# Reordering the sums, the row maxima and the score products inside a fused transformer block's attention

## The chip, the core and the metric

One core of a Trainium2 chip runs the whole kernel in one launch. Its engines each work through a queue of their own, in order: TensorE (PE, with its weight loads PEld), VectorE (DVE), ScalarE (ACT), GpSimd (POOL), and SyncE (SP), which issues DMAs. The metric is the device time of one execution in microseconds; less is better.

## The reference

A transformer block with adaptive layer norm, in float32: batch 2, 2048 tokens, width 512, 16 heads of 32, hidden width 2048. Six shift, scale and gate vectors per batch row come from a condition; then

```
xm = layernorm(x) * (1 + sc_a) + sh_a
q, k, v = split(xm @ Wqkv)
scores = where(causal, q @ k.T * 32**-0.5, -inf)
x = x + gt_a * (softmax(scores) @ v @ Wproj + bproj)
xm = layernorm(x) * (1 + sc_m) + sh_m
x = x + gt_m * (gelu(xm @ W1 + b1) @ W2 + b2)
```

The softmax is exact: each query's own maximum is subtracted before the exponential.

## The kernel before

The two batch rows run one after the other through three stages: queries, keys and values (written to DRAM, read back in another layout); attention; projection of the attention's output. The feed-forward half follows for both. The first row's stages take about the times 0 to 210, 210 to 735 and 735 to 800 us, the second's 800 to 970, 970 to 1490 and 1490 to about 1560.

**Units.** Attention works in 16 units per row: four groups of four heads (`c`), and in each four blocks of 512 queries (`i`), in the order 0, 1, 2, 3 for the first group and 0, 2, 1, 3 for the others. A unit has 4i + 3 steps: one per 128 keys that lie wholly before the block, then three for the diagonal. The first diagonal step (number 4i) has one key tile, the second two tiles (384 and 128 queries wide), the third one.

**A step** (`scores_t`). TensorE puts minus the row maxima into four PSUM banks `st`, one per head (`st<-fold,sel`), and adds keys times queries (`st<-qst,kst`). ScalarE takes the exponentials into a tile `e` (four buffers, `E_BUFS`). In diagonal steps GpSimd zeroes the triangle above the diagonal with one `affine_select` per key tile (the masks). Two steps later (`LAG`) TensorE multiplies by the values (`o<-e,vv`).

**Row sums.** The `e` tiles of four whole steps are added by GpSimd into a chain tile `ee` (VectorE does it in the last unit); the tile of the first diagonal step is added to the last chain. TensorE sums chains and diagonal tiles over keys (`sm<-ee,ones`, `sm<-e,ones`), a chain four steps after its last tile.

**Maxima ahead of time.** The maxima have to be known before a unit starts, so the same scores are computed once more beforehand, with queries on partitions (`s<-kst,qst`), in units up to `AHEAD` = 3 ahead. `Row.todo` lists these score products; an item is one bank: a whole key block for one query tile, a single diagonal tile, or a pair of diagonal tiles (128 and 384 keys, or 256 and 256). `Row.score(n)` takes n items, singles first or, with `late`, pairs first, looking at the next eight; `Row.bank` issues the products and then VectorE's reductions into `mx` (`tensor_reduce`, L500, or a masked reduction, L495). The products go to a pool `ps_s` of two PSUM banks, or, with `borrow`, to one of the four `st` banks (`st<-kst,qst`). `due` says how many items each step takes.

When a unit's items are done, `Row.split` (L517 to L521, five short VectorE operations) splits the maxima into three bfloat16 parts `mhl`, with a score bank as scratch. `Row.rows` transposes these (`ps_m`, in a bank of `ps_s`) and VectorE spreads the transpose into `fold`.

**What sets the order.** `mm` and `act` keep an instruction where the code has it on its engine. Other instructions, VectorE's reductions, splits and folds among them, are placed by the scheduler, as are SyncE's DMAs. The last unit also prepares the projection (`prepare`: multiplications on VectorE, L467, and GpSimd, L465), and `finish` stores a unit's values and sums. `project_phase` then loads the sums back, inverts them, loads tokens (`xt`) and the attention's output (`at`), multiplies `at` by the inverted sums on GpSimd (L1265) and projects (`ps_o`). Weights for the feed-forward are loaded in between (`Pieces.load`, L1153).

## Time and profile before

| | |
|---|---|
| time, median of 3 runs | 2315.55 us (2315.52 to 2318.34) |
| profiled execution, its time / its span | 2314.76 us / 2313.0 us |
| TensorE busy | 2252.9 us, 97% |
| VectorE, ScalarE, GpSimd busy | 1443.8, 1006.2, 1021.5 us |
| mean granted TensorE clock | 0.996 |
| GpSimd: sums `ee` (L656) | 106 and 42, 4.58 us each |
| GpSimd: masks (L643) | 128, 0.66 us each |
| VectorE: reductions of 512 scores (L500) | 768, 0.68 us each |
| ScalarE: exponentials (L635) | 1152, 0.58 us each |

In the rows of the profile, `out<-in` are the program's tile names, and the idle time in brackets is that of the engine just before, with what ended it.

### The profile page before, as it was taken

How to read it: one execution, taken by the hardware profiler on the slowest of the kernel's cores; microseconds unless marked ns; L12 is line 12 of the kernel's file. 1: busy time of each engine (PE TensorE's matmuls, PEld its weight loads, DVE VectorE, ACT ScalarE, POOL GpSimd, SP SyncE). 2: the span in 40 equal slices, each digit the busy share in tenths (PEclk: the TensorE clock that was granted, in tenths of full speed). 3: DMA queues.
4: the chain of work that ended last, by engine and by line, in shares of the span. 5: the costliest groups of instructions: out<-in, count | busy, mean ns of one | idle time of the engine just before them, and what ended most of it. 6: DMA issues, size and time to landing. Idle time of an engine off the chain costs nothing.

```text
span 2313.0 us, 32545 instructions
## 1 busy us (share of the span) xinstructions
PE 2252.9 (97%) x12033; PEld 1374.5 (59%) x12033; DVE 1443.8 (62%) x3025; ACT 1006.2 (44%) x1952; POOL 1021.5 (44%) x561
## 2 busy tenths in 40 slices
PE   7999999999999999999999999999999999999998
PEld 5777555555544588755555554344684585486477
DVE  4677766767757667777577766662573483375366
ACT  4434555555555244355555556513313322332320
POOL 7252986877782692278777879340000000000000
PEclk9999999999999999999999999999999999999999
DMA  9877143231323796523223123272354253353433
GB/s 302 279 259 195 37 92 69 65 83 47 99 94 128 258 300 230 162 67 78 71 72 88 47 74 114 98 254 86 118 165 150 99 174 130 116 171 121 153 113 131
DMA packets 160505, 311.52 MB, mean 135 GB/s; under 512 B 16545, under 2 KB 48845, under 8 KB 158553
## 3 DMA queue, kind: packets, MB, share of 16 engines
q1 hardware_dynamic: 155488, 285.53, 40.9%
q0 software_dynamic: 4480, 23.36, 2.6%
q8 instruction: 95, 1.56, 0.3%
q14 instruction: 66, 0.53, 0.1%
q10 hardware_dynamic: 376, 0.55, 0.1%
HBM read 229.95 MB, written 87.29 MB: 137 GB/s over the span
## 4 chain that ended last, share of the span: by engine, by line
PE 84%; POOL 6%; DVE 5%; issue 2%; ACT 1%; DMA 1%; SPq 0%; POOLq 0%; DVEq 0%; ACTq 0%
PE ps_a L206 24%; PE st L206 16%; PE ps_b L206 12%; PE o L206 9%; PE s L206 8%; PE ps_c L206 6%; POOL ee L656 4%; PE sm L206 4%; PE ps_o L206 2%; DVE junk L495 2%; PE ps_xt L214 1%; DVE mx L500 1%; ACT e L635 1%; PE ps_o L214 1%; POOL e L643 0%
## 5 line engine op out<-in xcount | busy, mean ns | idle before, releaser
L635 ACT ACTIVATE e<-st 128x512 f32<-128x512 f32 (+1 forms) x1152 | 571.5, 578 | 392.9 <-PE st L206 370.6
L500 DVE TENSOR_REDUCE mx<-s 128x1 f32<-128x512 f32 x578 | 381.6, 686 | 223.0 <-PE s L206 221.9
L656 POOL TENSOR_TENSOR ee<-ee,e 128x2048 f32<-128x2048 f32 x106 | 485.8, 4583 | 16.3 <-ACT e L635 9.0
L206 PE MATMUL st<-qst,kst 128*128 128x512 f32 (+3 forms) x1280 | 412.4, 388 | 0.0
L206 PE MATMUL s<-kst,qst 128*128 128x512 f32 (+3 forms) x1054 | 381.2, 393 | 10.7 <-DVE mx L500 6.1
L206 PE MATMUL ps_a<-sum,w 128*128 128x256 f32 (+1 forms) x1088 | 346.6, 454 | 0.0
L206 PE MATMUL o<-e,vv 128*32 128x512 f32 (+3 forms) x2560 | 293.7, 540 | 9.4 <-POOL e L643 9.3
L206 PEld LDWEIGHTS st<-qst,kst 128*128 128x128 f32 x1280 | 230.0, 189 | 100.6 <-issue 67.6
L206 PEld LDWEIGHTS ps_a<-sum,w 128*128 128x128 f32 x1088 | 206.3, 190 | 109.8 <-issue 91.4
L495 DVE CUSTOM_DVE_ANT_0 junk<-s,causal 128x128 bf16<-128x128 f32 (+3 forms) x476 | 224.9, 472 | 65.0 <-PE s L206 51.3
L656 POOL TENSOR_TENSOR ee<-e 128x2048 f32<-128x2048 f32 x42 | 192.5, 4583 | 138.9 <-ACT e L635 130.8
L206 PEld LDWEIGHTS s<-kst,qst 128*128 128x128 f32 x1054 | 196.0, 188 | 70.5 <-DVE mx L500 21.7
L1615 DVE TENSOR_TENSOR h<-c,ps_b 128x512 f32<-128x512 f32 x32 | 22.0, 688 | 202.4 <-PE ps_b L206 202.4
L206 PEld LDWEIGHTS <-sel 32*128 32x128 bf16 x1152 | 29.4, 91 | 196.2 <-issue 196.2
L500 DVE TENSOR_REDUCE mx<-st 128x1 f32<-128x512 f32 x190 | 129.6, 682 | 0.4
L643 POOL TENSOR_SCALAR_AFFINE_SELECT e<-e 128x512 f32<-128x512 f32 x128 | 82.1, 663 | 91.8 <-ACT e L635 89.6
L1789 ACT ACTIVATE h<-h,cols 128x512 f32<-128x512 f32 x96 | 69.3, 722 | 120.4 <-DVE h L1615 120.4
L206 PE MATMUL ps_b<-sum,w 128*128 128x256 f32 (+1 forms) x384 | 120.6, 450 | 0.0
L206 PE MATMUL st<-fold,sel 32*128 32x512 bf16 (+1 forms) x1152 | 117.5, 374 | 2.8 <-DVE mx L495 1.7
L206 PEld LDWEIGHTS o<-e,vv 128*32 128x32 f32 x2560 | 57.8, 109 | 96.2 <-issue 64.3
L984 POOL TENSOR_TENSOR lo<-lo,hi 128x512 fp32r<-128x512 f32 x32 | 40.8, 1276 | 132.4 <-ACT hi L982 130.7
L206 PEld LDWEIGHTS ps_b<-sum,w 128*128 128x128 f32 x384 | 73.0, 190 | 37.2 <-issue 30.6
(206 smaller groups left out, 3094.7 us busy)
## 6 DMA issues: line engine op xcount, KB each, us to landing
kst<-k SPq DMA_DIRECT2D x128, 256.0 KB
qst<-q SPq DMA_DIRECT2D x128, 256.0 KB
w<-w1d SPq DMA_DIRECT2D x32, 896.0 KB
w<-w2d SPq DMA_DIRECT2D x28, 1024.0 KB
w<-w2d SPq DMA_DIRECT2D x28, 768.0 KB
q<-hi SPq DMA_DIRECT2D x32, 256.0 KB
q<-lo SPq DMA_DIRECT2D x32, 256.0 KB
k<-hi SPq DMA_DIRECT2D x32, 256.0 KB
```

The costliest lines, as they stand in the source:

```text
L206: return tc.keep_in_program_order(nc.tensor.matmul(*args, **kw))
L214: return tc.keep_in_program_order(nc.tensor.transpose(dst, src, ident[:n, :n]))
L495: nc.vector.tensor_tensor_reduce(junk[:, :w], x, causal[:, QB - w :], 1.0, MASKED, ALU.add, ALU.max, m,)
L500: nc.vector.tensor_reduce(m, x, axis=AX.X, op=ALU.max)
L635: act(nc.scalar.activation(e4[:, h, :w], sts[h][:, :w], AF.Exp))
L643: nc.gpsimd.affine_select(d, d, pattern=[[0, HC], [1, P]], compare_op=ALU.is_ge, fill=0.0, base=0, channel_multiplier=-1,)
L656: act(nc.gpsimd.tensor_tensor(dst, x, y, ALU.add))
L984: engine.tensor_tensor(lo, d, hi.bitcast(F32), ALU.subtract)
L1615: act(nc.vector.tensor_tensor(dst, x, y, ALU.add))
L1789: nc.scalar.activation(d, ps, AF.Gelu, bias=col(r_b1 + half * HF + f, 1))
```

## The change

In the attention's steps every VectorE operation of the scores is now kept in the order of the code (`vector`). The split is put off to the end of the step (`settle`) and takes a score bank of its own there. The sum of the first diagonal tile is issued one step later. `score` takes pairs when the next items are mostly pairs, and steps with mostly pairs place one product early instead of two (`two_parts`).

```diff
 def score(self, n, borrow=None, late=False):
-                first = pairs if late else singles
+                many = len(pairs) > len(singles)
+                first = singles if lent or not (late or many) else pairs
...
                 self.bank(*item, s)
                 if not self.todo or self.todo[0][0] != u:
-                    self.split(u, self.mx, s)
+                    self.unsplit.append((u, self.mx))
                     self.mx = None
-                    self.at += 1
+                    if not self.paced:
+                        self.settle(s)
+
+        def settle(self, s=None):
+            for u, mx in self.unsplit:
+                if s is None:
+                    s = ps_sp.tile([P, QB], F32, tag="s", name="s")
+                self.split(u, mx, s)
+                self.at += 1
+                s = None
+            self.unsplit = []
+
+        def vector(self, ins):
+            return act(ins) if self.paced else ins
...
+        def two_parts(self):
+            own = [item for item in self.todo[:8] if item[0] == self.todo[0][0]]
+            return sum(len(parts) for _, _, parts in own) > len(own) * 3 // 2
...
 def scores_t(u, step, n):
-                sts = []
+                sts, early = [], 0
...
-                    if h < 2 and n >= 3 or h >= HC - n and n < 3:
+                    if n < 3:
+                        if h >= HC - n:
+                            row.score(1)
+                    elif h == 0 or h == 1 and not row.two_parts():
                         row.score(1)
+                        early += 1
...
                     row.score(1, st_bank)
-                    row.score(min(n, HC) - 3, late=True)
+                    row.score(min(n, HC) - 1 - early, late=True)
...
 in the loop over steps
                         if last:
                             row.score(row.count(cum[-1], u + 1))
+                    row.settle()
+                    if u + 1 < len(units) and row.rows_made == u + 1:
                         make_rows = last or (ready > u + 1 and n_step >= 1)
...
                     row.score(max(0, len(row.todo) - rest))
+                    row.settle()
...
+                    if i and n_step == i * TQ + 1:
+                        add_to(u, chain, single)
...
                     elif i and n_step == i * TQ:
-                        add_to(u, chain, es)
+                        single = es
                         sums_of, wait = (chain, False), 2
```

The reductions (L495, L500), the split's five operations and the fold are wrapped in `self.vector(...)`; `paced` is set at the start of a row's attention.

GpSimd's queue at the end of the fourth unit of the first row, before (`e_3256` is the tile of the first diagonal step, `e_3297` of the second, `e_3324` of the third):

```order
L656 TENSOR_TENSOR ee_3165<-ee_3165,e_3213 128x2048
L643 AFFINE_SELECT e_3256<-e_3256 128x4x128
L656 TENSOR_TENSOR ee_3165<-ee_3165,e_3256 128x2048
L643 AFFINE_SELECT e_3297<-e_3297 128x4x128 x2
L643 AFFINE_SELECT e_3324<-e_3324 128x4x128
```

and now (`e_3259`, `e_3300`, `e_3328`):

```order
L694 TENSOR_TENSOR ee_3168<-ee_3168,e_3216 128x2048
L681 AFFINE_SELECT e_3259<-e_3259 128x4x128
L681 AFFINE_SELECT e_3300<-e_3300 128x4x128 x2
L694 TENSOR_TENSOR ee_3168<-ee_3168,e_3259 128x2048
L681 AFFINE_SELECT e_3328<-e_3328 128x4x128
```

The sum stands behind the two masks of the second step, in all 22 units of this kind.

VectorE's queue where a unit's maxima are split in the third unit, before (`s_2587` is the bank of the unit's last pair, `s_2601`, `st_2609` and `s_2612` belong to the next unit):

```order
L495 ISA junk_2592,mx_2467<-s_2587,causal_68 128x384
L517 TENSOR_REDUCE s_2587<-mx_2467 128x16
L520 TENSOR_TENSOR mhl0_87<-s_2587,mhl0_87 128x4x4
L500 TENSOR_REDUCE mx_2602<-s_2601 128x1
L521 TENSOR_TENSOR mhl0_87<-s_2587,mhl0_87 128x4x4
L500 TENSOR_REDUCE mx_2602<-st_2609 128x1
L495 ISA junk_2615,mx_2602<-s_2612,causal_68 128x128
```

and now (rows between the split's own are left out in both):

```order
L497 ISA junk_2593,mx_2468<-s_2588,causal_68 128x384
L503 TENSOR_REDUCE mx_2598<-s_2597 128x1
L503 TENSOR_REDUCE mx_2598<-st_2605 128x1
L497 ISA junk_2613,mx_2598<-s_2608,causal_68 128x384
L521 TENSOR_REDUCE s_2615<-mx_2468 128x16
L527 TENSOR_TENSOR mhl0_87<-s_2615,mhl0_87 128x4x4
L503 TENSOR_REDUCE mx_2598<-s_2641 128x1
```

The split stands behind the reductions of the step and uses a bank of its own, `s_2615`.

SyncE's queue at the end of the first row's attention, before (`o_145` and `sum_130` are the last unit's values and sums in DRAM, the `W` rows are feed-forward weights):

```order
L1240 DMA qst<-wide_135 128x2048
L684 DMA o_145<-ot 128x512
L683 DMA sum_130<-sums 4x512
L1153 DMA qst<-in_L_cond_W_dram 128x2x128 x4
L373 DMA r<-sum_130 128x16
L1225 DMA xt<-in_x_dram 128x512 x6
L1234 DMA at<-o_143 128x2048
```

and now:

```order
L1283 DMA qst<-wide_135 128x2048
L1196 DMA qst<-in_L_cond_W_dram 128x2x128 x3
L722 DMA o_145<-ot 128x512
L721 DMA sum_130<-sums 4x512
L1196 DMA qst<-in_L_cond_W_dram 128x2x128
L1196 DMA vv<-in_L_cond_W_dram 128x2x128 x3
L374 DMA r<-sum_130 128x16
L1268 DMA xt<-in_x_dram 128x512 x6
L1277 DMA at<-o_143 128x2048
```

Three weight loads stand ahead of the two stores, and three more ahead of the loads behind them; in the second row's attention these rows stand as before.

More of the change, by code (lines that the diff above doesn't have):

```diff
@@ L306, in __init__ @@
             self.mx = None
+            self.unsplit, self.paced = [], False
             self.spent = 0
@@ L494, in bank @@
                     junk = bp.tile([P, QB], BF16, tag="junk", name="junk")
-                    nc.vector.tensor_tensor_reduce(
-                        junk[:, :w], x, causal[:, QB - w :],
-                        1.0, MASKED, ALU.add, ALU.max, m,
+                    self.vector(
+                        nc.vector.tensor_tensor_reduce(
+                            junk[:, :w], x, causal[:, QB - w :],
+                            1.0, MASKED, ALU.add, ALU.max, m,
+                        )
                     )
                 else:
-                    nc.vector.tensor_reduce(m, x, axis=AX.X, op=ALU.max)
+                    self.vector(nc.vector.tensor_reduce(m, x, axis=AX.X, op=ALU.max))
                 self.spent += cost(w, last)
@@ L516, in split @@
             )
-            nc.vector.tensor_reduce(m, mx, axis=AX.X, op=ALU.max)
-            nc.vector.tensor_reduce(hl[:, :, :, 0], mx, axis=AX.X, op=ALU.max)
-            nc.vector.tensor_tensor(r, m, hl[:, :, :, 0], ALU.subtract)
-            nc.vector.tensor_tensor(hl[:, :, :, 1], m, hl[:, :, :, 0], ALU.subtract)
-            nc.vector.tensor_tensor(hl[:, :, :, 2], r, hl[:, :, :, 1], ALU.subtract)
+            for ins in (
+                lambda: nc.vector.tensor_reduce(m, mx, axis=AX.X, op=ALU.max),
+                lambda: nc.vector.tensor_reduce(hl[:, :, :, 0], mx, axis=AX.X, op=ALU.max),
+                lambda: nc.vector.tensor_tensor(r, m, hl[:, :, :, 0], ALU.subtract),
+                lambda: nc.vector.tensor_tensor(
+                    hl[:, :, :, 1], m, hl[:, :, :, 0], ALU.subtract
+                ),
+                lambda: nc.vector.tensor_tensor(
+                    hl[:, :, :, 2], r, hl[:, :, :, 1], ALU.subtract
+                ),
+            ):
+                self.vector(ins())
         def count(self, upto, last_unit):
@@ L569, in rows @@
             )
-            nc.vector.tensor_tensor(
-                fold[u % 2].rearrange("p (t q) -> p t q", t=TQ + 1),
-                ps.unsqueeze(1).to_broadcast([P, TQ + 1, P]),
-                tmask.unsqueeze(2).to_broadcast([P, TQ + 1, P]),
-                ALU.mult,
+            self.vector(
+                nc.vector.tensor_tensor(
+                    fold[u % 2].rearrange("p (t q) -> p t q", t=TQ + 1),
+                    ps.unsqueeze(1).to_broadcast([P, TQ + 1, P]),
+                    tmask.unsqueeze(2).to_broadcast([P, TQ + 1, P]),
+                    ALU.mult,
+                )
             )
@@ L586, in attention_phase @@
         b, vv, kst, qst = row.b, row.vv, row.kst, row.qst
+        row.paced = True
         with pool(f"att{b}") as ap, pool(
```

## The prediction

> **What bounds the kernel now.** I read the page first, for the engine that is full; then the table of waits cut down to TensorE; then the timelines of TensorE, GpSimd, VectorE and SyncE around its longest waits.

> ```profile
> PE 2252.9 (97%) x12033; PEld 1374.5 (59%) x12033; DVE 1443.8 (62%) x3025; ACT 1006.2 (44%) x1952; POOL 1021.5 (44%) x561
> PE o L206 <- POOL e L643: 9.3, 8, 2.4
> PE s L206 <- DVE mx L500: 6.1, 10, 1.2
> PE s L206 <- DVE mx L495: 3.8, 9, 1.4
> PE st L206 <- DVE mx L495: 1.7, 4, 0.4
> ```

> TensorE is busy for 97%, and the change takes no matmul away, so it can give back only what TensorE loses by waiting. The last four rows (engine and tile, what was waited for, total, times, longest) are the waits that the edits aim at: 9.3 us for GpSimd's masks, 11.6 us for VectorE's maxima. The nearly full engine leaves no third source inside the attention.

> The 9.3 us sit in four places: the end of the fourth unit and of the last unit but one, in both batch rows. The first and third, GpSimd and ScalarE ahead of TensorE, with the twins of the second row behind:

> ```profile
> 338.47 2.06 ACT L635 ACTIVATE e<-st 128x512 f32<-128x512 f32 x4 [1.31 <-PE st L206]
> 340.72 4.55 POOL L656 TENSOR_TENSOR ee<-ee,e 128x2048 f32<-128x2048 f32 x1
> 345.23 2.40 POOL L643 TENSOR_SCALAR_AFFINE_SELECT e<-e 128x512 f32<-128x512 f32 x4
> 345.92 1.64 PE L206 MATMUL o<-e,vv 128*32 128x384 f32 x16 [1.90 <-POOL e L643]
> 350.15 1.06 PE L206 MATMUL sm<-ee,ones 128*32 128x512 f32 x8
> 351.90 0.61 PE L206 MATMUL o<-e,vv 128*32 128x256 f32 x8
> ...
> 1106.75 1.07 PE L206 MATMUL o<-e,vv 128*32 128x384 f32 x16 [1.63 <-POOL e L643]
> 1111.18 0.61 PE L206 MATMUL o<-e,vv 128*32 128x256 f32 x8
> ...
> 680.07 2.06 ACT L635 ACTIVATE e<-st 128x512 f32<-128x512 f32 x4 [0.95 <-PE st L206]
> 682.80 4.56 POOL L656 TENSOR_TENSOR ee<-ee,e 128x2048 f32<-128x2048 f32 x1
> 688.00 1.93 PE L206 MATMUL o<-e,vv 128*32 128x384 f32 x16 [2.43 <-POOL e L643]
> 695.15 0.60 PE L206 MATMUL o<-e,vv 128*32 128x256 f32 x8
> ...
> 1447.27 1.07 PE L206 MATMUL o<-e,vv 128*32 128x384 f32 x16 [2.43 <-POOL e L643]
> 1450.46 1.90 PE L206 MATMUL sm<-ee,ones 128*32 128x512 f32 x8
> 1453.06 0.60 PE L206 MATMUL o<-e,vv 128*32 128x256 f32 x8
> ```

> (Start, length, engine, line, operation; in brackets the idle time before.) In the first place the four exponentials of the second diagonal step end at 338.47 + 2.06 = 340.53. GpSimd is free at 340.7, but its queue holds the 4.55 us sum next and the two masks behind it, so the value products stand until 345.9. The waits also drag the clock down:

> ```profile
> 344.00:352.00 8.00, 6.10 (x58) 3.50 (x61) 0.82 (x1) 3.55 (x8) 4.50 (x7) 0.79 1.00 208
> 684.00:696.00 12.00, 9.57 (x76) 3.94 (x72) 2.50 (x4) 4.37 (x10) 5.12 (x4) 0.72 0.06 23
> 1104.00:1112.00 8.00, 6.37 (x74) 3.48 (x73) 0.82 (x1) 4.27 (x9) 5.57 (x7) 1.00 0.95 210
> 1444.00:1454.00 10.00, 7.57 (x68) 3.08 (x66) 2.50 (x4) 4.39 (x9) 4.40 (x4) 0.83 0.07 28
> ```

> Each row is a stretch with its length and the engines' busy times; the third figure from the end is the granted clock: 0.21 of 8 us, 0.28 of 12 and 0.17 of 10 are 1.7, 3.4 and 1.7 us lost behind three of the four waits, none behind the shortest.

> **The change, part by part.** *The sum behind the masks.* Only the order on GpSimd changes: two masks (0.6 us each, 2.40 over four) pass the sum. In the first place they run from 340.7 to 341.9, before TensorE gets there at 345.92 - 1.90 = 344.02, so nothing is waited for. What is late next is the sum: 341.9 + 4.6 = 346.5. Its reader, the row-sum product at 350.15, moves forward. The undisturbed copy (1106.75 to 1111.18, at full clock) takes 4.43 us from the first value product to the next, so the first place runs 344.02 to 348.45 instead of 351.90: **3.45 us**. Its row sum falls 1.75 us ahead of that, by the copy's spacing as by these rows (351.90 - 350.15), at 346.7, just behind the sum. In the second place only the wait goes, 1.63 us.

> In the third and fourth places the sum ends at 682.8 + 1.2 + 4.6 = 688.6. TensorE is ready at 685.57 and wants the row sum, by the fourth place, 1450.46 - 1447.27 = 3.19 us later, less the half of 1.7 us of lost clock that falls there: 2.4, so at 688.0. A new wait of 0.6 us stays. The clean length there is 1453.06 - 1447.27 - 1.7 = 4.1. Third: 695.15 - 685.57 - 4.1 - 0.6 = **4.9**; fourth: 1453.06 - 1444.84 - 4.1 - 0.6 = **3.5**. Together **13.5 us** (8.4 of waits, less 1.2 new, and 6.3 of clock). The other 18 units have no such wait to lose, and the tightest of them is

> ```profile
> 472.91 2.07 ACT L635 ACTIVATE e<-st 128x512 f32<-128x512 f32 x4 [1.81 <-PE st L206]
> 483.38 1.06 PE L206 MATMUL sm<-ee,ones 128*32 128x512 f32 x8
> ```

> where the sum would end 1.2 + 4.6 us after the exponentials' 474.98, at 480.8, 2.6 us before its product. I take nothing there: the sum's delay lies in GpSimd's idle time, 56% of the span. Uncovered, 18 x 1.2 = 22 us. The tile of the moved sum is also held a step longer; the exponential that reuses it comes three steps on and has the same cover.

> [...]

> *VectorE's order, and the split last.* The split of the row maxima (L517 to L521) stood between reductions that free score banks:

> ```profile
> 275.33 0.18 DVE L517 TENSOR_REDUCE s<-mx 128x16 f32<-128x16 f32 x1
> 275.94 0.68 DVE L500 TENSOR_REDUCE mx<-s 128x1 f32<-128x512 f32 x1
> 276.54 0.18 DVE L521 TENSOR_TENSOR mhl<-s,mhl 128x16 bf16<-128x16 f32 x1
> 276.68 0.55 PE L206 MATMUL s<-kst,qst 128*128 128x128 f32 x2 [1.17 <-DVE mx L500]
> ```

> The split scribbles in the score bank that it was computed from, so that bank came free only at 276.6. Now it has a bank of its own, behind the step's reductions; the next product finds its bank at 275.3. I take the 1.17 us in both rows, 2.3 us, and 1.2 of the remaining 9 us: **3.5 us**. Bounds: all 11.6 us of the four rows' VectorE part above; below, a bank taken per split, of only two, 26 splits (13 units a row are scored inside the attention) of 1.4 us (275.33 to 276.72), 36 us. I stay near the upper rows since every split now has a step to finish in. The folds stand behind up to two more masked reductions; that too is in the lower bound.

> *Pairs spread.* The same instructions in other steps; TensorE's cost is nil either way, and VectorE's load evens out. Nothing taken beyond the 1.2.

> *The last unit* (VectorE sums there). The multiplication of the step now runs ahead of the sum:

> ```profile
> 727.88 4.45 DVE L659 TENSOR_TENSOR ee<-ee,e 128x512 f32<-128x512 f32 x4 [0.53 <-POOL e L643]
> 734.56 0.64 PE L206 MATMUL o<-e,vv 128*32 128x256 f32 x8 [0.27 <-POOL e L643]
> ```

> It half fills VectorE's 0.53 us of idleness, and 0.27 us of TensorE's is spare: a loss of 0.3 us per row (0 to 1.1), **-0.6**.

> *SyncE's queue, moved by the scheduler.* At the first row's end three weight loads now stand ahead of the stores of the last sums:

> ```profile
> 735.96 0.32 SPq L684 DMA_DIRECT2D o<-ot  x1
> 741.11 1.92 SPq L1153 DMA_DIRECT2D qst<-in_L_cond_W_dram  x4
> 743.12 0.41 SPq L373 DMA_DIRECT2D r<-sum  x1
> 746.42 0.43 SPq L1234 DMA_DIRECT2D at<-o  x1
> 755.14 1.27 POOL L1265 TENSOR_TENSOR at<-at,qst 128x512 f32<-128x512 f32 x1 [7.17 <-DMA at<-o]
> 765.50 1.27 POOL L1265 TENSOR_TENSOR at<-at,qst 128x512 f32<-128x512 f32 x1
> 764.01 3.94 PE L206 MATMUL ps_o<-kst,at 128*128 128x512 f32 x8
> ```

> Those loads wait for GpSimd until 741.11, so the two stores leave at about 742.6 and 743.0. Behind them now stand one weight load and three more (0.5 us each, by 1.92 for four), and the reload of the sums: 745.6 for 743.12, so the load `at<-o` slips by about 2.5 us, and GpSimd's first multiplication, which waited 7.17 us for it, with it. TensorE wants the fourth product of its block at 764.01 + 3 x 0.86 = 766.6, GpSimd ends the fourth chunk at 766.77: no cover. **-2.6 us** (0 if the bytes land sooner, 6.6 if the whole slip of the stores comes through).

> The sum: 13.5 + 3.5 - 0.6 - 2.6 = **13.8 us**. The profiled execution took 2314.8 us (1.8 around its span); the median, 2315.55, is 0.8 above. 2315.6 - 13.8 = **2301.8**.

> **The rivals.** *The clock stays.* If the half rate is not caused by these waits, or the 2.6 us at 766 brings it back, the 6.3 us go: 2301.8 + 6.3 = 2308.1. For: 1.63 us brought none, so it's no simple threshold. Against: three drops, three places, all of them right at the waits.

> *SyncE's stores cost their whole slip:* 6.6 and a half-rate stretch of 1.7 for 2.6, 2307.5. For: DMA is dense there and the load already ended a wait. Against: the old stores were early by far.

> *VectorE's written order holds TensorE.* In-order, a reduction waiting for its product holds up one that is ready, and each split turns over one of two banks. Every step that lends a bank could pay, and the lent products count them:

> ```profile
> L206 PE MATMUL st<-kst,qst x226: 388/396/453, 213.0 to 1430.8; 128*128 128x512 f32 x113
> ```

> At 0.1 us each that is 22.6 us, and no gain from VectorE, 2301.8 + 3.5 + 22.6 = 2327.9. It decides from (10.3 + 4.6)/226 = 0.066 us per step. For: VectorE is 62% busy, more in these steps. Against: TensorE's own order is the written one, so products come in the order in which they are reduced.

> *The wait only moves to the row sums.* If GpSimd is behind by 3 us more than these rows show, the four waits return as waits for the sum: about 2313.

> **How the numbers follow.** Chances: forecast 0.60, clock 0.12, SyncE 0.14, moved wait 0.07, written order 0.07. About 0.2%, 4.6 us, is what a measurement of this kernel tells from no change. The first three are faster by more than that: with 0.01 for mixtures on the border taken off, 0.85; the moved wait and the border are the same, 0.08; 0.07 slower. The range runs from 2296.5 (13.8, plus 3 of VectorE's further waits and 2.6 if the stores are free) to 2310.5, above both dearer cases; about 0.19 is left out.

> **What would show it.** In the profile after: no row of the value products waiting for GpSimd's masks but some tenths at the ends of rows; granted clock 1.00 in the four windows; a wait for the sum of at most 1 us in the third and fourth; the split behind the reductions and no 1.17 us wait; one wait of about 2.6 us for `at` at the first row's third projection block. I am wrong if waits for VectorE's maxima grow past 15 us, or the half rate is still there.

## The result, and the profile after

The changed kernel took 2304.05 us in the median of four runs (2301.64 to 2307.01), the kernel before 2315.53 us: a ratio of 0.9953, 95% interval 0.9934 to 0.9972, so 11.5 us faster (6.5 to 15.3 by the interval). Its profiled execution took 2301.64 us, its span is 2299.9 us, 13.0 us under that of before. The forecast was 13.8 us.

The table of TensorE's waits in the profile after (engine, tile, what was waited for; total, times, longest):

```profile
PE s L206 <- DVE mx L503: 2.8, 4, 1.1
PE ps_m L597 <- DVE mx L497: 2.0, 2, 1.0
PE s L206 <- DVE mhl L527: 1.5, 6, 0.3
...
PE sm L206 <- DVE ee L697: 1.3, 2, 0.6
PE ps_o L206 <- POOL at L1308: 1.2, 1, 1.2
...
PE s L206 <- DVE mx L497: 0.9, 1, 0.9
...
PE sm L206 <- POOL ee L694: 0.8, 2, 0.4
...
PE o L206 <- POOL e L681: 0.2, 1, 0.2
```

The waits for GpSimd's masks went from 9.3 us to 0.2, those for VectorE's maxima (`mx`, three rows, 11.6 us) to 3.7. What is left of these stood in before too: 1.08 us in the first unit of each row, 0.3 in unit 13, and one wait ahead of the attention (0.91 us, before 1.37). Four rows are new: the transposition `ps_m` waits for a reduction, and three waits for sums and for the projection's `at`. The first place of the masks, and the third, on GpSimd's and TensorE's timelines of the profile after:

```profile
338.28 1.80 POOL L681 TENSOR_SCALAR_AFFINE_SELECT e<-e 128x512 f32<-128x512 f32 x3
340.06 4.55 POOL L694 TENSOR_TENSOR ee<-ee,e 128x2048 f32<-128x2048 f32 x1
...
342.22 1.07 PE L206 MATMUL o<-e,vv 128*32 128x384 f32 x16
...
682.93 1.07 PE L206 MATMUL sm<-ee,ones 128*32 128x512 f32 x8 [0.42 <-POOL ee L694]
```

Three masks now stand ahead of the sum, the value products at 342.22 wait for nothing, and in the third place 0.42 us of waiting for the sum is left. The same stretches by window (length, TensorE's, its weight loads', VectorE's, ScalarE's and GpSimd's busy time; the third figure from the end is the granted clock):

```profile
336.00:346.00 10.00, 9.74 (x81) 4.98 (x81) 1.31 (x8) 6.61 (x15) 9.79 (x7) 1.00 0.51 108
676.00:688.00 12.00, 11.43 (x108) 4.84 (x104) 3.54 (x7) 8.47 (x19) 7.46 (x6) 1.00 0.14 49
1090.00:1102.00 12.00, 11.74 (x104) 5.51 (x100) 2.54 (x9) 7.71 (x17) 10.82 (x8) 1.00 0.53 122
1430.00:1444.00 14.00, 13.43 (x120) 5.62 (x112) 5.00 (x9) 10.08 (x22) 8.01 (x6) 1.00 0.19 68
888.00:896.00 8.00, 7.19 (x30) 6.00 (x30) 3.60 (x9) 5.35 (x10) 1.27 (x1) 0.79 0.95 259
```

The four places run at full clock. The last row is a half-rate stretch that the profile of before doesn't have, in the second row's queries, keys and values. Next, the split and the new wait of the transposition, TensorE's timeline, then VectorE's:

```profile
274.74 0.55 PE L206 MATMUL s<-kst,qst 128*128 128x128 f32 x2
275.23 1.07 PE L206 MATMUL sm<-ee,ones 128*32 128x512 f32 x8
...
609.25 0.50 PE L206 MATMUL s<-kst,qst 128*128 128x128 f32 x2
610.74 0.22 PE L597 MATMUL ps_m<-identb,mhl 128*128 128x128 bf16 x1 [0.99 <-DVE mx L497]
...
610.60 0.08 DVE L497 DVE_READ_ACCUMULATOR2_ANT mx<- 128x1 f32 x1
610.72 0.20 DVE L521 TENSOR_REDUCE s<-mx 128x16 f32<-128x32 f32 x1
```

The products at 274.74, which stood 1.17 us for a bank, stand no more. But at 610.74 the transposition stands until the last reduction of the pair (610.60) is done. The last unit, VectorE and TensorE, and the end of the first row on SyncE, TensorE and GpSimd:

```profile
718.04 5.51 DVE L697 TENSOR_TENSOR ee<-ee,e 128x512 f32<-128x512 f32 x4 [0.53 <-POOL e L681]
723.61 0.62 PE L206 MATMUL sm<-ee,ones 128*32 128x512 f32 x1 [0.63 <-DVE ee L697]
...
730.65 1.41 SPq L1196 DMA_DIRECT2D qst<-in_L_cond_W_dram  x3
732.10 0.47 SPq L722 DMA_DIRECT2D o<-ot  x1
739.38 0.40 SPq L1277 DMA_DIRECT2D at<-o  x1
758.65 1.13 PE L206 MATMUL ps_o<-kst,at 128*128 128x512 f32 x2 [1.15 <-POOL at L1308]
747.00 1.28 POOL L1308 TENSOR_TENSOR at<-at,qst 128x512 f32<-128x512 f32 x1 [5.51 <-ACT qst L934]
```

**Where the 13 us came from.** To book the difference I took from the two traces when TensorE begins the first product of each unit (`st<-fold,sel`) and of each projection (`ps_o<-kst`), and the change of these differences from one place to the next. Units 4 and 15, in which the mask waits lie, are parted at their third step. Negative is time gained, both rows together, in us; the experiments stand beside it.

| place | after | sum alone | order alone | split alone | no pairs | no order |
|---|---|---|---|---|---|---|
| units 0 to 11 without the mask waits | -7.1 | +0.1 | +2.6 | -4.9 | -4.0 | -8.9 |
| mask waits at unit 4 | -4.3 | -4.1 | 0.0 | -1.4 | -4.1 | -4.3 |
| transposition in unit 12 | +2.8 | 0.0 | 0.0 | 0.0 | 0.0 | +2.8 |
| mask waits at unit 15 | -8.6 | -8.6 | -1.5 | -1.5 | -8.5 | -8.5 |
| rest of unit 15 | +2.4 | +2.4 | 0.0 | +0.6 | +2.4 | +2.4 |
| between the rows | +2.4 | +4.0 | +0.7 | -0.5 | -1.1 | +2.7 |
| start, units 13 and 14, end | -0.8 | +0.1 | +1.0 | -0.1 | +0.3 | +0.6 |
| span, against 2313.0 | -13.0 | -6.1 | +2.8 | -7.8 | -15.1 | -13.2 |

Each column is a single profile. The last two places before the span move by some us from run to run (loads and clock windows), and the mask waits by about 1.5 us with each half-rate window behind them. Units 0 to 11 repeat to 0.8 us: the kernel with the last unit's sum in its own step (below) has the same code there and gains 6.3.

### The profile page after: what moved, and what is told of

Read it like the earlier page. It is cut to its first block, busy times and chain, and to the rows that moved or that the text cites. A ratio compares the mean times of both kernels' runs of the same rounds, so it can differ in the third digit from the quotient of the medians.

```text
span 2299.9 us, 32555 instructions
## 1 busy us (share of the span) xinstructions
PE 2249.0 (98%) x12033; PEld 1374.7 (60%) x12033; DVE 1441.7 (63%) x3025; ACT 1007.2 (44%) x1952; POOL 1020.6 (44%) x561
## 5 line engine op out<-in xcount | busy, mean ns | idle before, releaser
L206 PE MATMUL st<-qst,kst 128*128 128x512 f32 (+3 forms) x1280 | 408.4, 385 | 0.0
L206 PE MATMUL s<-kst,qst 128*128 128x512 f32 (+3 forms) x1046 | 378.9, 393 | 5.7 <-DVE mx L503 2.8
L206 PE MATMUL ps_a<-sum,w 128*128 128x256 f32 (+1 forms) x1088 | 346.6, 454 | 0.0
L206 PE MATMUL o<-e,vv 128*32 128x512 f32 (+3 forms) x2560 | 293.4, 538 | 0.3 <-POOL e L681 0.2
L206 PEld LDWEIGHTS st<-qst,kst 128*128 128x128 f32 x1280 | 228.4, 188 | 97.1 <-issue 64.5
L206 PEld LDWEIGHTS ps_a<-sum,w 128*128 128x128 f32 x1088 | 206.3, 190 | 109.8 <-issue 91.4
L206 PEld LDWEIGHTS s<-kst,qst 128*128 128x128 f32 x1046 | 194.9, 188 | 65.2 <-DVE mx L503 15.4
L206 PEld LDWEIGHTS <-sel 32*128 32x128 bf16 x1152 | 29.4, 91 | 197.0 <-issue 197.0
L206 PE MATMUL ps_b<-sum,w 128*128 128x256 f32 (+1 forms) x384 | 120.6, 450 | 0.0
L206 PE MATMUL st<-fold,sel 32*128 32x512 bf16 (+1 forms) x1152 | 116.0, 372 | 1.2
L206 PEld LDWEIGHTS o<-e,vv 128*32 128x32 f32 x2560 | 58.2, 108 | 86.1 <-issue 67.6
L206 PEld LDWEIGHTS ps_b<-sum,w 128*128 128x128 f32 x384 | 73.0, 190 | 37.2 <-issue 30.6
```

Source lines behind the costliest of these rows:

```text
L206: return tc.keep_in_program_order(nc.tensor.matmul(*args, **kw))
```

## Experiments

**The sum alone.** The kernel before with these lines of the change only:

```diff
+                    if i and n_step == i * TQ + 1:
+                        add_to(u, chain, single)
...
-                        add_to(u, chain, es)
+                        single = es
```

> The kernel before with one part of the change: the sum of the first diagonal tile one step later; VectorE's order, the split and the choice of pairs as before. My theory (the four waits for GpSimd's masks and the half-rate stretches behind them come from the sum alone): these rows of before go, 12 to 13.5 us, the two last units lose about 1.2 us each because VectorE's sum now stands behind a multiplication, and VectorE's waits for score banks (1.17, 0.4, 0.2 us) stay as in before: span 2302 to 2304 for 2313.0. Rival, the clock: the half rate hangs on where a wait falls and not on these waits, then it is back elsewhere and the span is 2305 to 2309. Rival, the edits need each other: without VectorE's order TensorE waits elsewhere, span over 2309.

2307.89 us against 2314.63, ratio 0.997 (0.9958 to 0.9981), span 2306.9. Its waits:

```profile
PE s L206 <- DVE mx L500: 6.1, 10, 1.2
PE s L206 <- DVE mx L495: 3.9, 9, 1.5
...
PE ps_o L206 <- POOL at L1267: 2.0, 1, 2.0
...
PE o L206 <- POOL e L643: 0.4, 2, 0.2
```

The mask entry is the whole 12.7 us, VectorE's waits stand as in before (6.1, 3.9), and the last units lose the same 2.4. So the sum is the cause of the gain at the masks and of the loss in the last units. The span is 3 us over my theory's, in the range of the rival in which the half rate comes back elsewhere. That it did: the wait for `at` was 2.0 us here, and half-rate stretches followed it (granted clock 0.79 from 760 to 768 us) and the layer norm's wait between the rows (0.86 from 888 to 900 us).

**The pairs undone.** The changed kernel with the earlier rule:

```diff
-                many = len(pairs) > len(singles)
-                first = singles if lent or not (late or many) else pairs
+                first = pairs if late else singles
...
-                    elif h == 0 or h == 1 and not row.two_parts():
+                    elif h < 2:
```

> The changed kernel without the choice of pairs (two products placed early in every step, single tiles first), the sum's place and VectorE's order and late split kept. Theory A (the new 0.99 us wait of the transposition at 610.74 and 1365.21 comes from a pair that the new choice leaves to the last step of a unit): the two waits go and TensorE's order there is that of before, 1.5 us a row, 2.9 in all, and VectorE's gains stay: span about 2297. Theory B (the 0.4 and 0.2 us waits in units 6, 7, 10 and 11 of before went because of the pairs): they come back, 5.4 us in all, beside the 2.9 gained: about 2302.5. Theory C (the late split alone makes the wait): the wait stays, 2300.

2301.0 us, ratio 0.9938 (0.9926 to 0.995), span 2297.9. Both A and B hold: the transposition's 2.8 us go, and 3.1 of VectorE's 7.1 go with them. Within the attention the pairs were worth nothing on balance. The lower span comes from the stage between the rows (-1.1 for +2.4).

**The last unit's sum in its own step.** The changed kernel, with the addition at once where VectorE does it:

```diff
-                    if i and n_step == i * TQ + 1:
+                    if i and n_step == i * TQ + 1 and u < len(units) - 1:
...
                         single = es
+                        if u == len(units) - 1:
+                            add_to(u, chain, es)
```

> The changed kernel, but in the last unit of each row, where VectorE does the sums, the first diagonal tile is added in its own step as in before. Theory A (the last units lost 1.2 us each because the sum came behind a multiplication on VectorE and then ran beside GpSimd's masks at 1.1 to 1.8 us an operation instead of 0.68): the waits of 0.63 us for VectorE's sums go, 2.4 us, span about 2297.5. Theory B (the place of the multiplications and the contention with GpSimd set it, not the sum's step): no change, 2299.5 to 2300.5, the operations at 1.1 to 1.8 us as before.

2303.47 us, ratio 0.995 (0.9935 to 0.9966), span 2302.1, of which 3.2 us were lost in the first 210 us, where the units hadn't begun. VectorE's timeline in the last unit, and SyncE's behind it:

```profile
720.84 4.44 DVE L697 TENSOR_TENSOR ee<-ee,e 128x512 f32<-128x512 f32 x4 [0.53 <-POOL e L681]
...
728.91 0.32 SPq L722 DMA_DIRECT2D o<-ot  x1
...
734.07 1.92 SPq L1198 DMA_DIRECT2D qst<-in_L_cond_W_dram  x4
```

The four additions take 4.44 us instead of 5.51, the wait for them is gone, and so is the loss: 0.0 in the rest of unit 15 for +2.4. Theory A holds for the waits. Not expected: the stores `o<-ot` are ahead of the weight loads again, and the wait for `at` is gone. So the moved sum of the last unit, through the scheduler, was also what put SyncE's stores behind: the six kernels with it moved waited 0.6 to 2.1 us for `at`, the others not at all. The stage between the rows lost 2.4 us here all the same, by longer waits for ScalarE and a half-rate window.

**Waits of many lengths.** Additions on a scratch tile ahead of the first diagonal mask of twenty units:

```diff
+                if step == i * TQ:
+                    for w_pad in PADS.get((b, u), ()):
+                        act(
+                            nc.gpsimd.tensor_tensor(
+                                idle[:, :w_pad], idle[:, :w_pad], idle[:, :w_pad], ALU.add
+                            )
+                        )
```

> The changed kernel with additions on a scratch tile put on GpSimd ahead of the first diagonal mask of ten units in each row, 1.9 to 7 us long, so that TensorE waits some 1 to 3.4 us for the mask at twenty places, each of another length: 2300 plus about 44 us of waits, plus what the clock takes. Theory A (a fixed grid of windows of 3.41 us: a window at half rate follows one in which TensorE worked less than about 0.46 of full rate, so about 1.85 us idle inside one window): of the thirteen waits over 1.85 us eight or nine are followed by a half-rate window, the others straddle two windows, and the stretches begin at a whole number of 3.4134 us from each other; span about 2359. Theory B (the length of the wait alone decides, over about 1.8 us): all thirteen, whatever their place, span about 2366. Theory C (a wait of nearly a whole 3.4 us is needed): none or one, span about 2345.

The span was 2346.6 us. The waits came out shorter than meant, 0.75 to 2.75 us, 31.7 in all, so the three spans forecast can't be compared with it. Seven were of 1.83 us and more, and a half-rate stretch followed each (granted clock 0.57 or 0.72 over the 8 or 6 us that hold it); thirteen of 1.58 and less had none. Two of the stretches lasted two windows: 2299.9 + 31.7 + nine windows at 1.7 is 2346.9. Two of them, window by window (length, TensorE's busy time, granted clock, DMA share, GB/s):

```profile
342.39:345.80 3.41, 1.54 (x12) 1.00 0.15 30
345.80:349.21 3.41, 2.83 (x13) 0.50 0.87 204
349.21:352.63 3.42, 3.42 (x20) 0.50 1.07 213
352.63:356.04 3.41, 3.41 (x41) 1.00 0.85 170
482.33:485.74 3.41, 0.84 (x9) 1.00 0.50 103
485.74:489.15 3.41, 3.41 (x15) 0.50 1.03 223
489.15:492.57 3.42, 3.42 (x32) 1.00 1.07 224
```

The stretches begin at 345.80 and 485.74, a third at 1260.57: 41 and 268 times 3.4133 us from the first. So do those of before (18.61, 346.29, 687.62 and 1448.79 us, which are 96, 100 and 223 times 3.4133 us apart) and of after (47.07 and 890.16 us, 247 times). These twenty waits alone agree with B as well. What tells A from B is a wait of one length that falls differently on these windows: 2.52 us for the layer norm in before and with the sum alone, first before's two windows, then the other's:

```profile
892.42:895.83 3.41, 1.85 (x9) 1.00 0.96 220
895.83:899.25 3.42, 2.09 (x14) 1.00 1.07 210
```

```profile
889.95:893.37 3.42, 0.87 (x4) 1.00 1.04 215
893.37:896.78 3.41, 3.07 (x11) 0.50 1.05 255
```

In before the wait lay across two windows, with TensorE busy for 1.85 and 2.09 us of them, and no half rate came; in the other it lay in one, with 0.87 us busy, and the next ran at 0.50. B falls, and C too: half rate followed waits of 1.83 to 2.75 us. The 0.46 in A was my estimate. Measured, in the profiles of before and after from 20 to 2290 us: the five windows at full clock with TensorE idle for 1.89 us or more (to 2.84) were followed by half rate, and none of those with TensorE idle for 1.81 us or less.

**Order alone, and split alone.** The kernel before with VectorE's operations kept in order and the split in place; and with the split put off, in a bank of its own, and VectorE left to the scheduler. Against the changed kernel, both without the sum and the pairs:

```diff
-                    if not self.paced:
-                        self.settle(s)
+                    self.settle(s)
...
-            return act(ins) if self.paced else ins
+            return ins
```

(the first part for the order alone, the second for the split alone).

> The kernel before with one part of the change: VectorE's operations of the scores kept in the order of the code, the split still in place with the bank it was computed from. Theory A (the late split with its own bank takes away the 1.17 us waits, the order the waits of 0.2 to 0.4 us): the two waits of 1.17 us stay, units 0 to 3 take what they took, units 4 to 11 gain 0.5 to 1 us a row; the four mask waits stay: span 2311 to 2313. Theory B (order does it all): the 1.17 us go too, 2310 or less. Theory C (an order written out costs by itself, a reduction that waits holds up one that is ready): span over 2314, new waits of TensorE for mx.

> The kernel before with one part of the change: the split at the end of the step, in a score bank of its own, while the scheduler still orders VectorE; no pairs, no later sum. Theory A (the split's scratch in the product's bank was the cause of the 1.17 us waits): these go, 1.1 to 1.3 us a row in units 0 to 3, the rest as before: span 2310 to 2311. Theory B (only together with the written order, since the scheduler pulls the split up again): no change, 2313. Theory C (a bank for each split is missed by the products): span over 2314 with new waits of products or transpositions for a bank.

Spans of 2315.8 and 2305.2 us. The waits with the order alone:

```profile
PE s L206 <- DVE mhl L527: 4.8, 8, 0.8
PE st L206 <- DVE mx L503: 3.3, 6, 0.7
...
PE s L206 <- DVE mx L503: 2.8, 4, 1.1
...
PE s L206 <- DVE mx L497: 0.6, 1, 0.6
```

The order by itself costs 2.6 us in units 0 to 11, and the span lies where theory C has it. Its reason is shown only in part. TensorE waited 4.8 us for splits (`mhl`), 0.6 in the profile of before, and 3.3 for reductions that free an `st` bank; but its waits for reductions of score banks fell from 9.9 to 3.4. In units 0 to 11, unit 4 aside, its idle time rose by 1.4 us, from 10.3 to 11.7; the other 1.2 us lie in its busy time, and why is not known. The split by itself gains 4.9 us, in units 4 to 11 (2.4) as in units 0 to 3 (2.6): A, and twice its size. Its span is some 5 us under A's: 2.4 by units 4 to 11, and 3.0 since fewer half-rate windows followed the mask waits, which stayed. At the first of them TensorE stood for 1.95 us, longer than before's 1.90, and no half rate followed:

```profile
340.63:344.05 3.42, 2.04 (x16) 1.00 0.70 129
344.05:347.46 3.41, 2.85 (x33) 1.00 1.00 225
347.46:350.87 3.41, 3.41 (x48) 1.00 1.06 212
```

**The transposition ahead of the split.**

```diff
+                    if u + 1 < len(units) and row.rows_made == u + 1:
+                        if not last and ready > u + 1 and n_step >= 1:
+                            row.rows(u + 1)
                     row.settle()
```

> The changed kernel, but where a step both transposes the maxima of the next unit and splits those of a later one, the transposition is issued ahead of the split. Theory A (the 0.99 us waits of the transposition at 610.74 and 1365.21 come from the split: it takes one of the two banks, the transposition then gets the bank whose pair of products is not yet reduced): both waits go and 1.3 to 1.5 us a row with them, without touching the pairs: span about 2297. Theory B (the pair that lies late in the step is the cause, whatever the banks): the waits stay, 2300.

On TensorE's timeline there the transposition no longer waits:

```profile
611.36 0.50 PE L206 MATMUL s<-kst,qst 128*128 128x128 f32 x2
611.71 0.23 PE L597 MATMUL ps_m<-identb,mhl 128*128 128x128 bf16 x1
```

The loss in unit 12 fell from 2.8 to 0.6 us with the pairs left where they were, so the split ahead of the transposition was the cause: A. It takes the late pair as well, as the wait is also gone with the pairs undone. The span was 2308.2 all the same, since 10.8 us were lost between the rows: 2.1 for `at`, 3.5 and 3.0 for ScalarE (1.3 and 2.5 in before), and four half-rate windows (granted clock 0.91 from 760 to 780 us, 0.85 from 840 to 860). What sets off that stage is not settled (below).

**No written order.** The changed kernel with `return ins` in `vector`.

> The changed kernel without VectorE's written order: the scheduler places its reductions, splits and folds; the late split with its own bank, the pairs and the sum's place are kept. Theory A (the order by itself costs a little, as it did alone, and the split and the pairs bring VectorE's gain): units 0 to 11 gain 7.1 us over before or up to 1 more, the transposition's wait may go: span 2298 to 2300 with no disturbance between the rows. Theory B (the pairs' gain needs the written order): units 0 to 11 gain only the 4.9 us that the split gave alone, span 2301 to 2303.

Span 2299.8 us; units 0 to 11 gain 8.9 us, 1.8 more than with the order, where theory A had up to 1. So the order costs in company too, and the pairs don't need it: over the split alone they bring 4.0 us.

**Versions put together.** Three kernels with the last unit's sum in its own step and the transposition ahead of the split: with all the rest of the change, without the pairs, and without the written order.

> The changed kernel with the transposition ahead of the split and, in the last unit of each row, the first diagonal tile added in its own step as before. If the entries add up: 2.8 us for the transposition's waits, 2.4 for the last units and 1.2 for the wait of the projection (SyncE's stores stand ahead of the weight loads again), 6.4 under the changed kernel: span 2293 to 2296 by how the first 200 us fall, median about 2297.5, ratio to before 0.9925. If the gains only move on to the loads of the second row's tokens (the waits for x at 842 and 888 us): 2297 to 2299.

> The kernel with the later sum (but for the last unit), VectorE's order and the late split, the transposition ahead of the split, and no choice of pairs. If the entries add up: VectorE's units 0 to 11 gain 4.0 instead of 7.1 to 7.7, the transposition's wait has no pair to wait for, the rest as in the kernel with everything: 3 us over that one, median about 2301 to 2302. If the calmer stage between the rows of the kernel without pairs (1.1 us gained there, no half-rate window) comes with the pairs' absence: 2298 to 2299.

> The kernel with the later sum (but for the last unit), the late split, the pairs, the transposition ahead of the split, and VectorE's order left to the scheduler. If the written order only costs: the same as the kernel with everything or 1 us less, median 2297.5 to 2299. If the pairs need the order: 2 to 3 us more, 2301 to 2302.

| | median | ratio to before | interval |
|---|---|---|---|
| all the rest | 2298.93 us | 0.9933 | 0.9919 to 0.9946 |
| without pairs | 2301.7 us | 0.9936 | 0.9921 to 0.9952 |
| without order | 2297.58 us | 0.992 | 0.9906 to 0.9934 |

The first came out 1.4 us over what the entries add up to, in the range of gains that only move on; the other two came out as the entries had it. The intervals of the three overlap, so they are not told apart; the third's ends where that of the changed kernel begins (0.9934). In the third's profile units 0 to 11 gained 9.1 us and the transposition lost 0.6. In all three the last units still lost 1.3 us, where the sum's place alone had brought it to 0, with VectorE's four additions at 5.56 us for 4.44. The traces of the seven kernels that add this tile in its own step show where they part: VectorE's second addition and a mask of GpSimd begin within 0.05 us of each other. In seven of their last units the addition was first, by 0.01 or 0.02 us; it took 0.68 us, the mask 1.16, and nothing was lost. In the other seven, the six of these three kernels among them, the mask was first by 0.03 or 0.04 us; it took 0.64 us, the addition about 1.15, the fourth addition fell beside a multiplication of GpSimd, and 0.7 us was lost in each. What moves the two by so little was not looked for.

## Why the prediction came out right, step by step

- **The sum behind the masks: 13.5 us forecast, 12.9 measured** (4.3 + 8.6), and 12.7 with the sum alone. The waits and the remaining wait for the sum (0.42 us for 0.6) are as worked out, and the clock's share came back in full.
- **The clock.** The rival in which it stays fell: no half rate in the four places. But the reason given for the waits' cost was incomplete. 6.3 us of it was not a price of these waits as such, but of how they fell on the windows of 3.41 us: with the split alone two of the same waits cost 1.5 us less each. How many half-rate windows an execution of before has is partly luck, and I took them from one profile. TensorE did not stand idle throughout the windows ahead of the three drops: in them it was busy for 1.52, 1.36 and 1.52 us of 3.41 (before, from 342.87, 684.21 and 1445.38 us).
- **VectorE: 3.5 us forecast, 7.1 gained and 2.8 lost, 4.3 on balance.** That the size is near is luck, two errors that cancel. The step that failed is the sharing: "I take the 1.17 us in both rows, 2.3 us, and 1.2 of the remaining 9". Of those 9 us, 4 lie ahead of the attention or in units 0 and 13, and all but 0.5 of them stayed; the other 5, the short waits in units 6, 7, 10 and 11, went. The split alone brought 4.9; the pairs, for which I took nothing, another 4.0; the written order, which I counted among the gains, cost 1.8. And the lower bound of that paragraph, a bank taken per split out of two, was real: it struck in 2 splits of the 26, at 1.4 us each, where a transposition of the same step came behind with a late pair in the other bank.
- **The last unit: 0.6 us forecast, 2.4 measured.** Mis-sized. I counted 0.6 us for the multiplication that runs ahead. The additions themselves became slower, 5.51 us for 4.45, since more of them fell beside GpSimd's masks and multiplications (in the first row 1.77, 1.12, 1.11 and 1.75 us one by one, for 1.77, 0.68, 1.12 and 1.12).
- **SyncE: 2.6 us forecast, 1.15 measured as the wait for `at`.** The queue slipped as worked out: the load `at<-o` left at 739.38 for 746.42, 7.0 us earlier where TensorE was 9.3 earlier, so 2.2 of the forecast 2.5 us. But GpSimd's first multiplication slipped by only 1.1 (747.00 for 755.14), and was released by ScalarE and no longer by the load. The stage as a whole lost 2.4 us, the rest at the layer norm and its half-rate window. In the other kernels with this queue the wait for `at` was 0.6 to 2.1 us.
- **The written order as a rival** (22.6 us, slower): a cost was there, 2.6 us alone, 0.9 with the split (4.9 to 4.0) and 1.8 with the split and the pairs, so about a tenth or less of the price that I gave it. That a waiting reduction holds up a ready one is not shown to be the reason.
- **The median.** 2304.05 is 2.3 above the forecast, since the profiled execution was the fastest of the four; the others granted 0.998 and 0.997 of the clock in the mean, where it had 0.999.
- **The sum of the terms** came near partly by luck: the masks and the last unit brought 2.4 us less than forecast, VectorE 0.8 more, and 0.8 came at the start, in units 13 and 14 and at the end, for which nothing was forecast.

**Still open:** what makes the stage between the rows vary from -1.1 to +10.8 us against before. Half-rate windows are a part of it (none without the pairs, four in the worst). In the worst, ScalarE waited for a store of keys:

```profile
853.23 0.62 ACT L1028 CAST hi<-lo 128x512 fp32r<-128x512 f32 x1 [4.88 <-DMA k<-hi]
```

I did not take these stores off their queue, so that their queue is the cause is only argued.

## What to carry to other kernels

An operation that takes scratch from a small pool of banks cost 1.4 us here where the next user of that pool stood right behind it: with two banks, look for what rotates onto the busy one, and issue that first. When several edits come as one, book the difference place by place, since their gains and losses cancel in the total: here a written order that cost about 2 us travelled with a split that brought 5. And a step that is moved for one engine's sake should be checked in the one unit where another engine does it; what was right for GpSimd cost 2.4 us on VectorE, and a store's place in SyncE's queue.

## What the hardware showed that I had not expected

```profile
L697 DVE TENSOR_TENSOR ee<-ee,e x56: 673/681/1766, 687.2 to 1476.3; 128x512 f32<-128x512 f32 x56
L681 POOL TENSOR_SCALAR_AFFINE_SELECT e<-e x128: 627/635/1437, 213.5 to 1477.5; 128x512 f32<-128x512 f32 x128
```

  The long ones, 1.1 to 1.8 us for 0.68 and 1.1 to 1.4 for 0.64, are those in the last units, where VectorE's additions and multiplications of tiles run beside GpSimd's masks and multiplications; of two that began nearly together, the first kept its usual time. Beside VectorE's other work, the reductions of score banks above all, nothing of this shows: 77 of the other 120 masks ran wholly beside it, and none took over 0.65 us.
